# Token lists of a routed expert layer: slots by block and scattered token numbers in place of one-hot matmuls

## The chip, the cores and the metric

One core of a Trainium2 chip runs the whole kernel in one launch. The metric is the device time in microseconds, from the first to the last instruction of the program; lower is better. All times below are of this one core.

## What is computed

The input is x of shape (4, 256, 64, 64), float32. Three modulated deformable 3x3 convolutions (256 to 256 channels, each with a plain 3x3 convolution in front of it that gives two offsets and a mask for each of nine taps) run one after another with a relu, on a copy of x that is normalised over channels; their result is added to x. Then every pixel is a token of 256 values, and a mixture of eight experts is added to it:

```
for wo, bo, w, b in params:                      # three layers
    x = relu(deform_layer(x, wo, bo, w, b))
...
logits = xf @ gate_w + gate_b                    # xf: 16384 tokens, normalised
probs = softmax(logits)
top2_vals, top2_idx = top_k(probs, 2)
...
h = gelu(xf @ w1 + bb1);  y = h @ w2 + bb2       # each expert, hidden size 512
out = out + we[:, None] * y                      # we: the gate of a token, 0 outside its top 2
```

The reference runs each expert on all tokens; the kernel runs an expert only on the tokens that chose it.

## The kernel before, in words

**Blocks and taps.** A block is 512 pixels (eight image rows) of one image and one convolution layer: 3 layers, 4 images and 8 blocks of each make 96 blocks. The list of stages in `run` fixes their order: all of (layer 0, image 0), one block of (0, 1), all of (1, 0), one block of (0, 1), all of (2, 0), then the rest of (0, 1), and so on; a block is named (layer, image, block) here. `main_block` does a block in nine taps. In a tap `samples` issues four gathers from GpSimd (L524; each brings the four corner pixels, 4 KB, for 128 positions), VectorE blends them in two steps (L530, L535), ScalarE scales the result (L538), TensorE transposes it two pairs of samples later (`turn`, L553), ScalarE copies it (L556), and TensorE multiplies it with the tap's weights (`share`, L570). After nine taps ScalarE applies the relu (L601). Nine buffers hold gathered pixels.

**What is woven in.** Everything else is cut into steps, written as generators, and laid between the taps. `step` runs after each tap and advances two lists: `plans_side` holds the offset convolutions (`off_block`, L378 to L448), `side` holds the storing of pixel tables, the preparation of images 2 and 3 (`pre_block`, five steps: load, transpose at L463 and statistics, normalise at L81 and store, transpose back at L483) and the tokens of finished blocks (`tokens`, seven steps). The steps of a list are spread over what is left of the block: with n steps left and r taps left, ceil(n / r) are taken. A step marked `after(self.last)` stands behind the newest L535 on its engine, `after(self.gathered)` behind the newest gather on GpSimd's queue, `after(self.turned)` behind the newest transpose on TensorE.

**The expert layer** is cut into five groups: images 0, 1 and 2 whole (32 sets of 128 tokens each), image 3 in two halves. A group passes through three lanes, `routes`, `tiles` and `sums`, each of which holds pieces with a price in taps; `pump` gives every lane one tap of credit after each tap, and a lane pops a piece when it has its price.
- `routes`: when the last block of a group has given its gates, `route` (L714 on) counts the tokens of each expert with two matmuls over all sets, gives each expert whole tiles of 256 tokens and at most one of 128, and each token a slot in the sorted order (`slots`). Then `invert` turns slots into the list of tokens, one set a piece: VectorE makes two one-hot matrices for each of the two choices (L836, L838), and TensorE multiplies them into one PSUM accumulator (`inv`, L842), which is copied to `tok` at L847. Pieces: 0 taps for `route`, 3 for the first set, 0.5 for each of the other sets (31, or 15 in a half), 3 for `begin`.
- `tiles`: for each tile of the list GpSimd fetches the expert's weights if they changed (L861) and the tokens' rows by one indirect gather for 128 tokens (L874); TensorE transposes them and does the two matmuls with a gelu between (L904, L918, L928, L936); VectorE adds the bias (L955), and the result goes to DRAM. A tile of 256 tokens costs 5.0, 6.0, 2.0, 1.5 or 0.0 taps by group (`pace`), one of 128 half of that.
- `sums`: for each set, GpSimd gathers both results of its tokens (L981), VectorE adds them with their gates (L996), TensorE transposes (L1014), and the output is stored.

After the last block, `settle` and `drain` pop what is left without regard to taps: `settle` one step of each list and one piece of tiles in turn, `drain` three pieces of tiles for one tap of credit of the routes and two of the sums.

Of the kernel before, what the change touches and what calls it, by code (L numbers as in the profile page):

```python
# [8 lines left out]
F32 = mybir.dt.float32  # L9
I32 = mybir.dt.int32  # L10
# [31 lines left out]
NW = 3  # L42
LEAST = 2.0**-30
# [14 lines left out]
def normalise(nc, pool, src, dst, eps, nm):  # L58
# [16 lines left out]
    for _ in range(3):  # L75
        nc.vector.tensor_tensor(sq, rs, rs, ALU.mult)
        nc.vector.scalar_tensor_tensor(sq, sq, -0.5, ve, ALU.mult, ALU.mult)
        nc.vector.scalar_tensor_tensor(rs, sq, 1.5, rs, ALU.add, ALU.mult)
    yield rs
    for t in range(T):  # L80
        nc.vector.tensor_scalar(  # L81
            dst[:, t, :], src[:, t, :], mv[:, t, 0:1], rs[:, t : t + 1], ALU.subtract, ALU.mult
        )


class Group:


    def __init__(self, b, n0, n1):
# [8 lines left out]
        self.zt, self.acc, self.gy, self.sums, self.py = {}, [], [], [], None  # L98
        self.order = [self.starts[s % NW] + s // NW for s in range(self.NF)]
# [26 lines left out]
class Weave:  # L126
# [3 lines left out]
    def __init__(self, ctx, tc, ins, out):  # L130
# [29 lines left out]
        self.side, self.plans_side = [], []  # L160
# [58 lines left out]
    def ffn_constants(self):  # L219
# [9 lines left out]
        for g in self.groups:  # L229
            g.zd = self.dram.tile([g.M * P, C], F32, name=f"z_{g.nm}", tag=f"z_{g.nm}")  # L230
        self.ys = [
# [28 lines left out]
        self.fresh = {}  # L260
        for M in {g.M for g in self.groups}:
            fresh = cst.tile([P, E, M], F32, name=f"fresh_{M}")
            nc.vector.memset(fresh, 1.0)
            nc.vector.memset(fresh[:, :, 0:1], 0.0)
            self.fresh[M] = fresh
# [10 lines left out]
        self.token = {}  # L276
        for M in {g.M for g in self.groups}:
            assert M * P // 2 <= 2048
            token = cst.tile([P, M], F32, name=f"token_{M}")
            nc.vector.tensor_scalar(  # L280
                token, self.row_f[:, :M], float(P), self.part, ALU.mult, ALU.add
            )
            nc.vector.tensor_scalar(token, token, float(M * P // 2), None, ALU.subtract)
            self.token[M] = token


# [163 lines left out]
    def pre_block(self, b, n, wins, spare, spill=0):  # L450
# [19 lines left out]
        rest = normalise(nc, self.small, h, h, EPS_C, nm)  # L470
# [140 lines left out]
    def tokens(self, b, n, r):  # L611
# [4 lines left out]
        if n == grp.n0:  # L616
            grp.cw = self.rt2.tile([P, 2, grp.M], F32, tag="cw", bufs=3, name=f"cw_{grp.nm}")
            grp.rk = self.rt2.tile([P, E, grp.M], F32, tag="rk", name=f"rk_{grp.nm}")
        xc = self.big.tile([P, CC, BLK], F32, tag="a", name=f"xr_{nm}")
# [32 lines left out]
        rest = normalise(nc, self.small, tok, z, EPS_T, nm)  # L652
# [54 lines left out]
        for i in range(2):  # L707
            w = small("lg", (P, TPB, E))
            nc.vector.scalar_tensor_tensor(w, rk, float(i), pr, ALU.is_equal, ALU.mult)
            nc.vector.tensor_reduce(grp.cw[:, i, m0 : m0 + TPB], w, AX.X, ALU.add)  # L710
        if n == grp.n1 - 1:
            self.enqueue(grp)

    def route(self, grp):  # L714
# [6 lines left out]
        def small(tag, shape, dt=F32):  # L721
            return self.rt.tile(list(shape), dt, tag=tag, name=f"{tag}_{grp.nm}")

        both = small("r0", (P, E, M))
        nc.vector.tensor_scalar(both, grp.rk, 1.0, None, ALU.is_le)
        rp = self.ps.tile([P, 2, E, M], F32, tag="tp", name=f"rp_{grp.nm}")
        nc.tensor.matmul(rp[:, 0], lhsT=self.upper, rhs=both, start=True, stop=True)
        nc.tensor.matmul(rp[:, 1], lhsT=self.ones, rhs=both, start=True, stop=True)
        tot = small("r1", (P, E, M))
        nc.vector.tensor_copy(tot, rp[:, 1])  # L730
        slot = small("r2", (P, E, M))
        nc.vector.tensor_tensor_scan(
            slot.rearrange("p e m -> p (e m)"),
            self.fresh[M].rearrange("p e m -> p (e m)"),
            tot.rearrange("p e m -> p (e m)"),
            0.0, ALU.mult, ALU.add,
        )

        ni = small("ni", (P, E), I32)
        nc.vector.tensor_scalar(ni, slot[:, :, M - 1], float(P - 1), None, ALU.add)  # L740
# [8 lines left out]
        for v in range(2):  # L749
# [11 lines left out]
        cut = small("cut", (P, E))  # L761
        nc.vector.tensor_scalar(cut, nt[:, 0], float(FT), None, ALU.mult)
        nc.vector.tensor_tensor(off[:, 1], off[:, 1], cut, ALU.subtract)
        nc.vector.tensor_tensor(off[:, 1], off[:, 1], off[:, 0], ALU.subtract)
        nc.vector.tensor_scalar(end[:, 0], end[:, 0], float(FU), None, ALU.mult)
        nc.vector.tensor_scalar(end[:, 1], end[:, 1], base, None, ALU.add)
        nc.vector.tensor_tensor(slot, slot, tot, ALU.subtract)
        nc.vector.tensor_tensor(slot, slot, rp[:, 0], ALU.add)
        every = [P, E, M]
        over = small("r1", (P, E, M))  # L770
        nc.vector.tensor_tensor(over, slot, cut.unsqueeze(2).to_broadcast(every), ALU.is_ge)
        nc.vector.tensor_tensor(
            over, over, off[:, 1].unsqueeze(2).to_broadcast(every), ALU.mult
# [3 lines left out]
            slot, slot, off[:, 0].unsqueeze(2).to_broadcast(every), ALU.add  # L777
# [9 lines left out]

# [6 lines left out]
        part = small("exv", (P, NF))  # L794
        for v in range(2):
            past = small("r1", (P, NF, E))
            nc.vector.tensor_tensor(
                past,
                first.unsqueeze(2).to_broadcast([P, NF, E]),
                end[:, v].unsqueeze(1).to_broadcast([P, NF, E]),  # L800
                ALU.is_ge,
            )
            nc.vector.tensor_reduce(part if v else ex, past, AX.X, ALU.add)
        nc.vector.scalar_tensor_tensor(ex, ex, float(E), ex, ALU.is_lt, ALU.mult)
        nc.vector.tensor_tensor(ex, ex, part, ALU.add)
# [9 lines left out]
        nc.vector.tensor_copy(grp.wrow, rows)  # L815


        grp.digits = []
        for v, (op, k) in enumerate(((ALU.bitwise_and, P - 1), (ALU.logical_shift_right, 7))):
            di = small("di", (P, 2, M), I32)  # L820
            nc.vector.tensor_scalar(di, grp.slots, k, None, op)
            df = small(f"df{v}", (P, 2, M))
            nc.vector.tensor_copy(df, di)
            grp.digits.append(df)
        grp.inv = self.ps1.tile([P, grp.NU], F32, tag="py", name=f"inv_{grp.nm}")

    def invert(self, grp, m):


        nc = self.nc  # L830
        lo, hi = grp.digits
        n = grp.NU
        for i in range(2):
            nm = f"{grp.nm}_{m}_{i}"
            at = self.ffn.tile([P, P], F16, tag="at", name=f"at_{nm}")
            nc.vector.tensor_scalar(at, self.row_f, lo[:, i, m : m + 1], None, ALU.is_equal)  # L836
            num = self.ffn.tile([P, n], F16, tag="num", name=f"num_{nm}")
            nc.vector.tensor_scalar(  # L838
                num, self.row_f[:, :n], hi[:, i, m : m + 1], self.token[grp.M][:, m : m + 1],
                ALU.is_equal, ALU.mult,  # L840
            )
            nc.tensor.matmul(  # L842
                grp.inv, lhsT=at, rhs=num,
                start=(m == 0 and i == 0), stop=(m == grp.M - 1 and i == 1),
            )
        if m == grp.M - 1:
            nc.vector.tensor_scalar(  # L847
                grp.tok, grp.inv, float(grp.M * P // 2), None, ALU.add
            )
# [176 lines left out]
    def enqueue(self, grp):  # L1026

        put = self.routes.put
        put(0, lambda: self.route(grp))
        for m in range(grp.M):  # L1030
# [181 lines left out]
```

## Time and profile before

| | us |
|---|---|
| median of 3 runs (lowest, highest) | 6431.33 (6419.34, 6440.2) |
| the profiled execution: its own time | 6426.59 |
| the profiled execution: span of its instructions | 6424.5 |

| engine | busy us (share of the span) |
|---|---|
| PE, matmuls | 5903.1 (92%) |
| DVE (VectorE) | 4954.5 (77%) |
| POOL (GpSimd) | 4396.0 (68%) |
| PEld, weight loads | 3413.5 (53%) |
| ACT (ScalarE) | 3298.7 (51%) |

2247.56 MB pass through the DMA engines, at a mean of 350 GB/s. A busy share is a mean over the span. The profile also gives the busy time of every engine, the TensorE clock that was granted, the DMA engines' busy share and their rate for any stretch of the span, and blocks can be told apart in it by the times of L601, the last instruction of each.

### The profile page before, as it was taken

How to read it: one execution, taken by the hardware profiler on the slowest of the kernel's cores; microseconds unless marked ns; L12 is line 12 of the kernel's file. 1: busy time of each engine (PE TensorE's matmuls, PEld its weight loads, DVE VectorE, ACT ScalarE, POOL GpSimd, SP SyncE). 2: the span in 40 equal slices, each digit the busy share in tenths (PEclk: the TensorE clock that was granted, in tenths of full speed). 3: DMA queues.
4: the chain of work that ended last, by engine and by line, in shares of the span. 5: the costliest groups of instructions: out<-in, count | busy, mean ns of one | idle time of the engine just before them, and what ended most of it. 6: DMA issues, size and time to landing. Idle time of an engine off the chain costs nothing.

```text
span 6424.5 us, 88218 instructions
## 1 busy us (share of the span) xinstructions
PE 5903.1 (92%) x26358; PEld 3413.5 (53%) x26358; DVE 4954.5 (77%) x11575; ACT 3298.7 (51%) x7154; POOL 4396.0 (68%) x4215
## 2 busy tenths in 40 slices
PE   7999999889899999999889999999987999987987
PEld 3444444444455555665445555555643566644675
DVE  7988888888977768888877877778988764678621
ACT  3555555555555555555455555555654544454422
POOL 4666776666777767667777776767777764667644
PEclk8999999899999999999999999999999999999998
DMA  8999999999899999999899999999999996899854
GB/s 286 388 370 378 408 404 401 377 361 365 325 393 372 366 340 399 391 355 364 315 356 366 393 380 352 385 368 380 387 369 345 346 338 235 322 335 341 314 179 145
DMA packets 799851, 2247.56 MB, mean 350 GB/s; under 512 B 102184, under 2 KB 300456, under 8 KB 790544
## 3 DMA queue, kind: packets, MB, share of 16 engines
q0 software_dynamic: 550240, 1971.12, 81.2%
q1 hardware_dynamic: 249136, 270.82, 12.3%
q8 instruction: 212, 3.47, 0.2%
q14 instruction: 263, 2.15, 0.1%
HBM read 2166.72 MB, written 191.81 MB: 367 GB/s over the span
## 4 chain that ended last, share of the span: by engine, by line
PE 67%; DVE 11%; DMA 10%; issue 5%; ACT 4%; POOL 2%; SPq 0%; DVEq 0%; ACTq 0%; POOLq 0%
PE acc L570 33%; PE tp L553 9%; DMA g<-tab,idx 8%; PE ph L918 7%; PE py L936 7%; PE po L378 6%; DVE g L530 4%; DVE s L535 3%; ACT s L538 2%; PE pm L392 1%; POOL g L524 1%; PE lp_tok L642 1%; ACT win L601 1%; PE ftp L904 1%; PE tpv L338 1%
## 5 line engine op out<-in xcount | busy, mean ns | idle before, releaser
L524 POOL DMA_INDIRECT g<-tab,idx x3456 | 3625.0, 1049 | 1553.5 <-issue 595.8
L570 PE MATMUL acc<-sT,wk 128*128 128x512 f32 x6912 | 3319.7, 602 | 3.7 <-ACT r L601 1.9
L530 DVE SCALAR_TENSOR_TENSOR g<-g,cf 128x512 f32<-128x512 f32 x3456 | 2561.0, 744 | 348.6 <-DMA g<-tab,idx 341.1
L535 DVE SCALAR_TENSOR_TENSOR s<-g,cf 128x256 f32<-128x256 f32 x3456 | 1656.9, 482 | 480.5 <-PE tp L553 181.0
L538 ACT ACTIVATE s<-s,cf 128x256 f32<-128x256 f32 x3456 | 1664.0, 509 | 642.2 <-DVE s L535 593.8
L570 PEld LDWEIGHTS acc<-sT,wk 128*128 128x128 f32 x6912 | 1195.8, 194 | 818.0 <-issue 801.3
L556 ACT COPY sT<-tp 128x512 f32<-128x512 f32 x1728 | 1011.3, 586 | 1180.0 <-PE tp L553 1167.1
L553 PEld LDWEIGHTS tp<-ident,s 128*128 128x128 f32 x6912 | 867.8, 143 | 1220.0 <-ACT s L538 684.8
L553 PE MATMUL tp<-ident,s 128*128 128x128 f32 x6912 | 1225.1, 282 | 273.0 <-ACT s L538 269.6
L918 PE MATMUL ph<-fzT,w 128*128 128x256 f32 (+1 forms) x2688 | 590.2, 356 | 13.4 <-ACT fzT L908 10.6
L936 PE MATMUL py<-w,hT 128*128 128x256 f32 x2328 | 583.5, 387 | 16.4 <-ACT hT L928 10.4
L918 PEld LDWEIGHTS ph<-fzT,w 128*128 128x128 f32 x2688 | 450.2, 192 | 126.7 <-ACT hT L928 33.5
L928 ACT ACTIVATE hT<-ph,w 128x256 f32<-128x256 f32 (+1 forms) x672 | 266.2, 442 | 467.1 <-PE ph L918 306.2
L936 PEld LDWEIGHTS py<-w,hT 128*128 128x128 f32 x2328 | 425.4, 192 | 136.4 <-issue 47.3
L874 POOL DMA_INDIRECT zt<-z,tok x291 | 292.7, 1006 | 132.4 <-issue 59.2
L981 POOL DMA_INDIRECT gy<-ys,slots x256 | 276.6, 1081 | 105.5 <-issue 65.9
L955 DVE TENSOR_TENSOR y<-py,w 128x512 f32<-128x512 f32 (+1 forms) x168 | 103.3, 615 | 305.2 <-PE py L936 296.7
L861 POOL DMA_INDIRECT w<-in_W,wrow x168 | 177.8, 1059 | 216.9 <-ACT hT L928 45.9
L378 PE MATMUL po<-win,wo 128*32 128x504 f32 (+2 forms) x2560 | 323.8, 551 | 1.5 <-ACT om L387 0.7
L996 DVE SCALAR_TENSOR_TENSOR ta<-gy,cw,ta 128x256 f32<-128x256 f32 x256 | 121.6, 479 | 106.5 <-DMA gy<-ys,slots 87.1
L378 PE MATMUL po<-win_pre,wo 128*32 128x504 f32 (+2 forms) x1280 | 172.0, 572 | 4.0 <-ACT om L387 3.4
L378 PEld LDWEIGHTS po<-win,wo 128*32 128x32 f32 x2560 | 73.1, 109 | 192.0 <-issue 150.1
(171 smaller groups left out, 2836.4 us busy)
## 6 DMA issues: line engine op xcount, KB each, us to landing
tab<-hv SPq DMA_DIRECT2D x512, 128.0 KB
g<-tab,idx POOLq DMA_INDIRECT x3456
tab<-h_pre SPq DMA_DIRECT2D x128, 256.0 KB
ys<-y SPq DMA_DIRECT2D x123, 256.0 KB
wk<-in_conv_w SPq DMA_DIRECT2D x117, 256.0 KB
xc_pre<-in_x SPq DMA_DIRECT2D x32, 512.0 KB
xr_tok<-in_x SPq DMA_DIRECT2D x32, 512.0 KB
t<-t_tok SPq DMA_DIRECT2D x32, 512.0 KB
```

Source lines behind the costliest of these rows:

```text
L378: nc.tensor.matmul(po[g * Q : (g + 1) * Q, :].rearrange("q (r w) -> q r w", w=W)[:, r0:r1, x0:x1], lhsT=self.wo[l][:, 3 * ky + kx, c, :], ...
L524: self.gathered = nc.gpsimd.indirect_dma_start(out=g.rearrange("p x s f -> p (x s f)"), out_offset=None, in_=self.table(*self.stages[i][:2 ...
L530: nc.vector.scalar_tensor_tensor(g[:, :, 0, :], g[:, :, 1, :], cf[:, j, 0:1], g[:, :, 0, :], ALU.mult, ALU.add,)
L535: self.last = nc.vector.scalar_tensor_tensor(s, g[:, 1, 0, :], cf[:, j, 1:2], g[:, 0, 0, :], ALU.mult, ALU.add)
L538: nc.scalar.activation(s, s, AF.Copy, scale=cf[:, j, 2:3])
L553: self.turned = nc.tensor.transpose(tp[:, c, u * P : (u + 1) * P], ss[u][:, c * P : (c + 1) * P], self.ident)
L556: nc.scalar.copy(self.sT[:, :, t0 * P : (t0 + 2) * P], tp)
L570: nc.tensor.matmul(self.acc[:, o, :], lhsT=self.wk[k][:, c, o * P : (o + 1) * P], rhs=sT[:, c, :], start=(k == 0 and c == 0), stop=(k == K ...
L874: self.nc.gpsimd.indirect_dma_start(out=zt, out_offset=None, in_=grp.zd, in_offset=bass.IndirectOffsetOnAxis(ap=grp.tok[:, j : j + 1], axi ...
L918: nc.tensor.matmul(ph[:, h, :n], lhsT=w1[:, o : o + P], rhs=zT[:, c, :n], start=(c == 0), stop=(c == CC - 1),)
L936: nc.tensor.matmul(py[:, u, :], lhsT=hT[h // 2][:, h % 2, u * P : (u + 1) * P], rhs=w2[:, h * C : (h + 1) * C], start=(h == 0), stop=(h == ...
L981: self.nc.gpsimd.indirect_dma_start(out=g, out_offset=None, in_=self.ys[grp.i % 3], in_offset=bass.IndirectOffsetOnAxis(ap=grp.slots[:, i, ...
```

## The change

1. Each expert gets a region of 4096 entries in a table in DRAM (`ids`; two tables in turn). After the gates of a block, a new generator `place` (six steps, in a list of its own, `place_side`) counts that block's tokens per expert with two small matmuls, adds the running count `full`, and writes the numbers of the block's tokens into their experts' regions: eight indirect DMAs of GpSimd, each with 128 destinations of 4 bytes, in two steps of four.
2. `route` works out tiles from `full`, moves slots from the regions to the sorted order, works out which 128 entries of `ids` each unit of the list reads, and reads all of them by one indirect gather; one transpose gives `tok`. It is a generator in six pieces, of 0, 1, 1, 1, 1 and 1 taps; `begin` costs 1 tap. `invert`, its one-hot matrices and its matmuls are gone.
3. The normalising step of `pre_block` runs on ScalarE (a scale and a bias for each position) once the startup is over; in the startup, and for the tokens, it stays on VectorE.
4. `pre_block` steps get a list of their own (`pre_side`), one step a tap. `settle` empties the new lists too.
5. The paces become 6.0, 7.5, 2.4, 1.5 and 0.0 taps.

The diff, cut to its core:

```
-def normalise(nc, pool, src, dst, eps, nm):
+def normalise(nc, pool, src, dst, eps, nm, scalar):
...
+    if scalar:
+        away = pool.tile([P, T], F32, tag="away", name=f"away_{nm}")
+        nc.vector.scalar_tensor_tensor(away, mv[:, :, 0], -1.0, rs, ALU.mult, ALU.mult)
     yield rs
     for t in range(T):
...
+        if scalar:
+            nc.scalar.activation(
+                dst[:, t, :], src[:, t, :], AF.Identity,
+                bias=away[:, t : t + 1], scale=rs[:, t : t + 1],
+            )
...
+        for ids in self.ids:
+            nc.gpsimd.dma_start(ids.rearrange("(p a) b -> p (a b)", p=P), nought)
...
+        self.aside(6, self.place(grp, n), place=True)
+
+    def place(self, grp, n):
...
+        both = small("lg", (P, E, TPB))
+        with self.after(self.last):
+            nc.vector.tensor_scalar(both, rk, 1.0, None, ALU.is_le)
+        yield
+        rp = self.ps.tile([P, 2, E, TPB], F32, tag="tp", name=f"rp_{nm}")
+        with self.after(self.turned):
+            nc.tensor.matmul(rp[:, 0], lhsT=self.upper, rhs=both, start=True, stop=True)
+            nc.tensor.matmul(rp[:, 1], lhsT=self.ones, rhs=both, start=True, stop=True)
+        up = small("rp", (P, 2, E, TPB))
+        nc.scalar.copy(up, rp)
+        yield
+        cs = small("pr", (P, E, TPB))
+        with self.after(self.last):
+            nc.vector.tensor_tensor_scan(
...
+        for t in range(TPB):
+            if t % 2 == 0:
+                yield
+            for i in range(2):
+                with self.after(self.gathered):
+                    ins = nc.gpsimd.indirect_dma_start(
+                        out=ids,
+                        out_offset=bass.IndirectOffsetOnAxis(ap=put[:, i, t : t + 1], axis=0),
+                        in_=self.token[:, m0 + t : m0 + t + 1],
+                        in_offset=None,
+                    ).ins
...
-    def invert(self, grp, m):
...
-            nc.vector.tensor_scalar(at, self.row_f, lo[:, i, m : m + 1], None, ALU.is_equal)
...
-            nc.tensor.matmul(
-                grp.inv, lhsT=at, rhs=num,
...
+        lists = small("r0", (P, P))
+        with self.after(self.gathered):
+            ins = nc.gpsimd.indirect_dma_start(
+                out=lists[: grp.NU],
+                out_offset=None,
+                in_=self.ids[grp.i % 2].rearrange("(n a) b -> n (a b)", a=P),
+                in_offset=bass.IndirectOffsetOnAxis(ap=line[: grp.NU, 0:1], axis=0),
+            ).ins
...
+            nc.tensor.transpose(tp, lists[: grp.NU, :], self.ident[: grp.NU, : grp.NU])
+        with self.after(self.last):
+            nc.vector.tensor_scalar(grp.tok, tp, float(M * P - 1), None, ALU.min)
...
-        put(0, lambda: self.route(grp))
-        for m in range(grp.M):
-            put(0.5 if m else 3, lambda m=m: self.invert(grp, m))
-        put(3, lambda: self.begin(grp))
+        gen = self.route(grp)
+        for taps in range(6):
+            put(min(1, taps), lambda: next(gen, None))
+        put(1, lambda: self.begin(grp))
...
-        for side, taps in ((self.plans_side, K), (self.side, 4 if short else K)):
+        for side, taps in (
+            (self.plans_side, K), (self.side, 4 if short else K), (self.pre_side, K),
+            (self.place_side, K + k),
+        ):
...
-        for i, (g, pace) in enumerate(zip(self.groups, (5.0, 6.0, 2.0, 1.5, 0.0))):
+        for i, (g, pace) in enumerate(zip(self.groups, (6.0, 7.5, 2.4, 1.5, 0.0))):
...
-                        self.aside(5, self.pre_block(1, m, rows.setdefault((-1, 1), {}), True))
+                        gen = self.pre_block(1, m, rows.setdefault((-1, 1), {}), True)
+                        self.aside(5, gen, pre=True)
```

## The prediction

> **What bounds the kernel now.** I read the page first, then the busy time by stage, with block ends taken from L601's times, then the waits and the timeline of the stages that stood out. On the page, PE is busy 92% of the span and the DMA engines close to all of it:
>
> ```profile
> PE   7999999889899999999889999999987999987987
> ...
> DMA  8999999999899999999899999999999996899854
> PE 67%; DVE 11%; DMA 10%; issue 5%; ACT 4%; POOL 2%; SPq 0%; DVEq 0%; ACTq 0%; POOLq 0%
> ```
>
> PE is full in the middle and drops at a few places. The stages, by windows (us, then PE, PEld, DVE, ACT, POOL busy, granted clock, DMA share, GB/s):
>
> ```profile
> 619.00:1018.80 399.80, 370.15 (x1512) 183.60 (x1512) 348.97 (x662) 234.29 (x498) 285.32 (x289) 1.00 1.03 406
> 1186.20:1556.00 369.80, 328.09 (x1396) 182.15 (x1396) 323.52 (x910) 196.61 (x417) 236.25 (x216) 0.91 0.97 363
> 1625.60:1745.00 119.40, 102.84 (x462) 50.06 (x462) 111.29 (x314) 60.37 (x126) 93.50 (x72) 0.97 0.90 326
> 1987.20:2462.10 474.90, 468.81 (x2067) 276.98 (x2066) 354.59 (x671) 256.54 (x578) 339.22 (x330) 1.00 0.97 364
> 3034.90:3250.10 215.20, 174.74 (x766) 88.11 (x766) 185.48 (x543) 97.03 (x203) 164.03 (x134) 0.91 0.89 316
> 3518.30:3977.10 458.80, 451.94 (x1967) 260.55 (x1966) 355.97 (x674) 253.50 (x562) 329.71 (x325) 1.00 0.98 374
> 4450.90:4614.70 163.80, 160.75 (x684) 99.82 (x684) 146.91 (x338) 102.20 (x215) 120.65 (x118) 1.00 1.00 380
> 4725.20:4850.70 125.50, 97.15 (x356) 50.13 (x356) 108.07 (x248) 62.31 (x127) 98.00 (x91) 0.96 0.99 371
> 4725.20:5048.40 323.20, 255.74 (x976) 129.19 (x976) 284.10 (x723) 156.29 (x315) 254.23 (x225) 0.95 0.96 353
> 5774.70:5909.80 135.10, 101.74 (x394) 53.40 (x394) 125.19 (x362) 62.25 (x127) 105.52 (x91) 0.94 0.94 345
> ```
>
> Row 1 is eight blocks of (1,0), convolution alone: 50.0 us a block at a DMA share of 1.03, so DMA-bound, with 46.3 us of PE. Rows 4 and 6 are (1,1) and (1,2), with experts: 59.4 and 57.4 a block, PE at 98.6%, so PE-bound. Row 6 fetches 24 units of 128 tokens, 1.5 tiles a block: a tile of 256 costs (56.5 - 46.3) / 1.5 = 6.8 us of PE. Rows 3, 5, 9 and 10 are stages between experts: lists are made, sums are loaded, and PE stands idle 17, 40, 67 and 33 us at a clock of 0.91 to 0.97. So the expert work is crowded into PE-bound blocks, while other blocks wait for DMA and DVE.
>
> **1. The inverts go.** They are 85.5 + 76.0 us of DVE (L838, L836) and 40.1 of PE (L842), all in these stages. Row 3 is blocks (0,1,3) and (0,1,4): DVE is busy 93%, 41.1 us of it inverts, and they slow the gathers' issue beside them:
>
> ```profile
> 1625.60:1745.00 119.40, 92.09 (x71) 0.97 0.90 326
> 1987.20:2462.10 474.90, 294.44 (x286) 1.00 0.97 364
> ```
>
> That is L524 on POOL: 1.30 us each against 1.03. Without inverts I take such a block at 55 us, near (0,1,1), 55.8. Taking all 41.1 us off would pass the DMA bound of 50. In the new order of the instructions, the first list is read in (0,1,3), and its experts start in (0,1,4), about a block earlier: the way to the experts takes 12 taps (six of `place`, six of the lane) instead of 21.5 (3 + 31 x 0.5 + 3). Row 3: 55 + 55 + two tiles at 2 (below) = 114, **-6**.
>
> **2. Experts are spread.** Counting units of 128 tokens by block in GpSimd's two orders, 25 units (12.5 tiles) move out of PE-bound blocks into (0,1,4), (2,1,7) to (0,2,4) and (2,2,5) to (1,3,1). Between (0,1,5) and (2,1,6) 11 units leave, 5.5 x 6.8 = **-37**; between (1,2,3) and (2,2,5), six units, **-20**. Where they arrive, PE has 5 to 16 us idle a block and pays nothing until that is used (then 6.8 a tile again); DMA pays 256 KB of rows, 256 KB of results and about 0.37 MB of weights (1.18 MB, some 11 changes in 35.5 tiles): 0.9 MB at 400 GB/s, 2.2 us. What the exchange gives can be seen side by side: rows 7 and 8 are blocks of one layer, (2,2,1) to (2,2,3) with 1.67 tiles each, 54.6 us, and (2,2,6), (2,2,7) with sums instead, 62.8.
>
> **3. Sums move.** They follow the tiles, so group 1's leave row 9's blocks for (1,3,3) on, where PE sets the pace (DMA share 0.86 from 5048.4 to 5443.4). Row 9 becomes 54.6 x 2 for (2,2,6) and (2,2,7), about 60 for (1,3,0), 56 for (1,3,1), 53 for (1,3,2), with its inverts gone too: 278, **-45**. At (2,1,7) to (0,2,4), 60.0 and row 5's 215.2: experts now go on there (65, as (2,1,2)), and sums and inverts go: 65 + 72 + 57 + 62 = 256, **-19**. From (0,2,5) to (1,2,2), 433 us, all seven blocks get sums: four at 65, three at 60.5, 441, **+8**. (1,3,3) to (2,3,3) keeps its 71 units; it gains 18 sets of sums, 18 x 0.375 us of L1014 = 7 us of PE, and loses the idle time of its last two blocks: 0. Row 10: no inverts, **-11**; the tail starts some four units ahead: **-5**.
>
> **4. Preparation.** Row 2 is six blocks of (2,0), 61.6 us each, and each has one gap:
>
> ```profile
> 1314.19 1.88 PE L570 MATMUL acc<-sT,wk 128*128 128x512 f32 x4
> 1322.04 1.94 PE L483 MATMUL tp_pre<-ident,h_pre 128*128 128x128 f32 x8 [5.96 <-DVE h_pre L81]
> ```
>
> In the old order, L81 and L483 fall in one tap, because tokens and preparation share a list of 12 steps. The new order has 24 transposes L553 between the forward and the backward transpose, not 16: half a tap, 3.3 us, more room. Moving L81 itself saves 4 x 0.41 us of DVE and adds four ACT instructions of about 0.6 (L538's 0.51 plus 0.1 for a bias operand, L387's 687 ns against L556's 586); ACT stands at 51%, L483 and the stores on SP's queue wait for ACT then, up to 1 us longer. By the row, 5.96 shrinks by 3.3. The Trainium skill, TensorE: Matmul & The Clock Gate (Part 1), says that an idle window of about 3.4 us halves the clock. The trace agrees (0.51 at 1321.4:1324.8, 0.50 at 1335.1:1341.9), so a gap below it would also spare half of 10.2 us: by the rule 8.4 us a block. But 22 MB a block keep DMA at 0.97, so the block can't fall below about 58 (61.6 x 0.97 / 1.03). From 61.6 I take 58.4, for (2,0,1) to (2,0,7): **-22**.
>
> **5. What is added.** For each of 32 blocks: 13 small DVE operations (L709 201 ns, L710 179, L677 191), 2.4 us, against 1.5 saved by step 4; two small matmuls, about 0.5 us as L642's 272 ns; one ACT copy, 0.19; eight scatters. `route` keeps some 50 small operations, in pieces a tap apart. A scatter takes GpSimd about 1.0 us, whatever the rows' size (L874 1006 ns with 1 KB rows, L861 1059 with 9 KB): 8 us a block on POOL, which has about 20 us free a block in row 2. Four stand together ahead of the next gather, and each waits for the DMA eight places before it: four gathers, 4 x 1.25 us, are still in the rings, as long as the four issues take, so DMA need not run dry. DVE's scan waits for ACT's copy of PE's counts; samples queue behind it. It stands one tap later, and L535 waits for PE today for 1.1 us (181.0 in 159 waits).
>
> What 128 writes of 4 bytes to DRAM cost the rings, no row shows: the smallest DRAM writes here are 1 KB. Below: their bytes, nothing (128 x 4 against a gather's 512 KB). Above: the Trainium skill, DMA: Bandwidth & Descriptors (Latency and other measured facts), gives tiny transfers a round trip of at least some 0.8 us to HBM, and its Specifications make writes under 512 B read-modify-writes. If each scatter held the rings so long, 256 x 0.8 = 205 us. I take 0.8 us for a block in all, near the lower end, since the closest rows (gathers of 1 KB pieces) pass at the rate of the large ones: **+25**. The clearing of `ids` is 256 KB at the start: nothing.
>
> **The sum.** -6 -37 -20 -45 -19 +8 -11 -5 -22 +25 = -132. From the profiled execution, 6426.6 - 132 = 6295; it lies 5 us under the median of the runs, so **6295** stands against either. A check: from 1556 to 5048 PE is idle 213 us; the sum leaves about 110, some 2 us a block, as the PE-bound blocks have now.
>
> **The rivals.** *The spread doesn't pay* (chance 0.19): blocks with sums run at a DMA share of 0.95 to 0.99, so tiles that arrive cost there what they save elsewhere. In favour: (0,2,5) to (0,3,0) have sums and experts, and take 67 us. Then only inverts (-12 for each of three groups, -11 in row 10), step 4 and step 5 count: -47 - 22 + 25 = -44, 6383. Against: rows 7 and 8.
> *Slower: the scatters hold the rings* (0.14). They share the rings with the gathers, whose data the chain waits for. At 0.8 us each they cost 205, not 25: 6475. It decides from (132 + 25) / 256 = 0.61 us a scatter on.
> *It doesn't do what it says* (0.07): DVE's waits in `place` stall the samples and lists come no sooner. At L535's longest wait of 4.9 us in each block, 157 us more, less what overlaps: about 6430, no change.
> The sum itself has 0.60.
>
> **Chances and range.** A measurement can tell about 0.3%, 19 us. Faster by more: the sum, the first rival and a little of the third, 0.81. Within: 0.05. Slower: 0.14. The range reaches down to 6200 (scatters free, -25; the clock's whole gain, -45; two us more in each freed block) and up to 6415, past the first rival; what it leaves out is mostly the scatters' case.
>
> **What would show it.** Right: PE at 97% or more from 1750 to 4900 with no stage under 90%; (2,2,6) and (2,2,7) near 55 us; L483's gap in (2,0) under 3 us at a clock above 0.95; L524 near 1.03 us in (0,1,3). Wrong: DVE waiting longer for gathers just after scatters, block times over 62 us in (2,0), or POOL waits for scatters that hold gathers back. Then the range's upper part, or the second rival, is the case.

## The result and the profile after

| | us |
|---|---|
| before, median of 4 runs | 6429.82 |
| after, median of 4 runs (lowest, highest) | 7331.23 (7323.67, 7332.36) |
| ratio, 95% interval | 1.1406 (1.1392 to 1.1419) |
| the profiled execution after: its time, its span | 7330.78, 7328.6 |

The changed kernel is 901 us slower; the forecast was 135 us faster, and its range ended at 6415. The page after, the busy tenths of TensorE, its clock, the DMA engines and their rate, then the chain that ended last:

```profile
PE   7999996567899997677888999986668999856767
...
PEclk9999998788999998888999999997888999977888
DMA  9999999998999999899899999998898998898975
GB/s 319 388 359 396 409 403 289 217 258 262 334 370 390 367 388 274 218 261 284 291 365 370 388 366 382 373 333 239 230 255 278 335 336 300 242 217 206 265 142 171
...
PE 50%; DMA 25%; DVE 11%; issue 6%; POOL 4%; ACT 4%; DVEq 0%; SPq 0%; POOLq 0%; ACTq 0%
PE acc L583 25%; DMA g<-tab,idx 14%; DMA ids<-token,put 8%; PE tp L566 7%; PE po L391 5%; PE ph L1005 5%; PE py L1023 5%; DVE g L543 4%; DVE s L548 3%; POOL ids L779 2%; POOL g L537 2%; ACT s L551 1%; PE pm L405 1%; DMA zt<-z,tok 1%; ACT win L614 1%
```

DMA went from 10% of the chain to 25%, and the scatters (`ids<-token,put`, where `put` is the tile with a block's destinations) are 8% by themselves. In the slices ahead of the tail where PE falls to 5 or 6, the DMA row still says 8 or 9 while the rate is 206 to 289 GB/s: packets are open and move little. Those slices are the stages that route tokens. By stages (us, then PE, PEld, DVE, ACT, POOL busy, clock, DMA share, GB/s), the rows are (1,0); (2,0,2) to (2,0,7); (0,1,3) and (0,1,4); (1,1); (2,2,1) to (2,2,3); (2,2,6) to (1,3,2):

```profile
612.10:1012.80 400.70, 370.56 (x1512) 183.41 (x1512) 349.16 (x661) 234.39 (x498) 284.88 (x289) 1.00 1.03 407
1183.70:1746.50 562.80, 359.02 (x1416) 188.28 (x1416) 340.77 (x959) 206.18 (x446) 282.06 (x266) 0.80 0.90 239
1829.70:1975.70 146.00, 118.12 (x467) 62.29 (x467) 102.17 (x246) 64.66 (x137) 98.73 (x98) 0.91 0.92 319
2209.30:2660.90 451.60, 447.41 (x1961) 258.44 (x1960) 355.76 (x675) 249.97 (x562) 332.89 (x325) 1.00 1.00 381
...
4862.30:5125.60 263.30, 179.27 (x659) 106.37 (x660) 159.81 (x381) 102.63 (x213) 136.20 (x132) 0.81 0.91 248
...
5303.60:5714.20 410.60, 296.00 (x1105) 168.72 (x1105) 256.07 (x602) 168.06 (x347) 243.97 (x237) 0.85 0.90 268
```

Blocks without scatters do what was forecast: (1,0) is unchanged, and (1,1) takes 451.6 where it took 474.9. Most blocks with eight scatters take 80 to 130 us where they took 53 to 91: six blocks of (2,0) 562.8 for 369.8. VectorE's wait for gathers before (us in total, times, longest), then the waits after, and then what the trace says of the scatter's line:

```profile
DVE g L530 <- DMA g<-tab,idx: 341.1, 406, 10.8
```

```profile
DVE g L543 <- DMA g<-tab,idx: 1383.1, 613, 28.4
...
POOL g L537 <- DMA ids<-token,put: 317.3, 63, 13.4
...
POOL ids L779 <- DVE put L772: 196.8, 30, 11.4
```

```profile
L779 POOL DMA_INDIRECT ids<-token,put x256: 967/992/1482, 1181.8 to 7028.1; - x128
...
  DVE put L772: 196.8, 30
  DMA ids<-token,put: 179.2, 48
```

VectorE waited 341.1 us for gathers before, at most 10.8 at a time; now 1383.1, up to 28.4. The issue of a scatter takes the 1.0 us that was assumed (median 992 ns). Three new waits stand beside it: gathers wait on GpSimd for scatters to land, scatters wait for scatters, and in 30 of the 32 blocks that scatter GpSimd waits for the scatter's indices, 6.6 us on average.

### The profile page after: what moved, and what is told of

It reads as the page before. It is cut to its first block, busy times and chain, and to the rows that moved or that the text cites. A ratio compares the mean times of both kernels' runs of the same rounds, so it can differ in the third digit from the quotient of the medians.

```text
span 7328.6 us, 88233 instructions
## 1 busy us (share of the span) xinstructions
PE 6058.4 (83%) x26215; PEld 3470.0 (47%) x26215; DVE 4931.1 (67%) x11385; ACT 3361.0 (46%) x7294; POOL 4569.5 (62%) x4478
## 4 chain that ended last, share of the span: by engine, by line
PE 50%; DMA 25%; DVE 11%; issue 6%; POOL 4%; ACT 4%; DVEq 0%; SPq 0%; POOLq 0%; ACTq 0%
PE acc L583 25%; DMA g<-tab,idx 14%; DMA ids<-token,put 8%; PE tp L566 7%; PE po L391 5%; PE ph L1005 5%; PE py L1023 5%; DVE g L543 4%; DVE s L548 3%; POOL ids L779 2%; POOL g L537 2%; ACT s L551 1%; PE pm L405 1%; DMA zt<-z,tok 1%; ACT win L614 1%
## 5 line engine op out<-in xcount | busy, mean ns | idle before, releaser
L537 POOL DMA_INDIRECT g<-tab,idx x3456 | 3538.4, 1024 | 1809.4 <-issue 632.2
L543 DVE SCALAR_TENSOR_TENSOR g<-g,cf 128x512 f32<-128x512 f32 x3456 | 2569.6, 744 | 1390.7 <-DMA g<-tab,idx 1383.1
L583 PE MATMUL acc<-sT,wk 128*128 128x512 f32 x6912 | 3397.9, 615 | 8.2 <-ACT r L614 5.8
L566 PE MATMUL tp<-ident,s 128*128 128x128 f32 x6912 | 1263.7, 287 | 798.1 <-ACT s L551 786.9
L566 PEld LDWEIGHTS tp<-ident,s 128*128 128x128 f32 x6912 | 892.9, 147 | 1806.8 <-ACT s L551 1229.9
L583 PEld LDWEIGHTS acc<-sT,wk 128*128 128x128 f32 x6912 | 1231.7, 199 | 894.5 <-issue 872.2
L1005 PE MATMUL ph<-fzT,w 128*128 128x256 f32 (+1 forms) x2688 | 617.3, 366 | 32.9 <-ACT fzT L995 18.6
L1023 PE MATMUL py<-w,hT 128*128 128x256 f32 x2328 | 600.3, 391 | 37.0 <-ACT hT L1015 20.3
L779 POOL DMA_INDIRECT ids<-token,put x256 | 267.4, 1045 | 437.7 <-DVE put L772 196.8
L1068 POOL DMA_INDIRECT gy<-ys,slots x256 | 257.4, 1005 | 144.8 <-issue 68.6
L995 ACT COPY fzT<-ftp 128x512 f32<-128x512 f32 (+1 forms) x168 | 89.0, 530 | 207.7 <-PE ftp L991 204.4
```

Of the source, the lines that this page charges most:

```text
L537: self.gathered = nc.gpsimd.indirect_dma_start(out=g.rearrange("p x s f -> p (x s f)"), out_offset=None, in_=self.table(*self.stages[i][:2 ...
L543: nc.vector.scalar_tensor_tensor(g[:, :, 0, :], g[:, :, 1, :], cf[:, j, 0:1], g[:, :, 0, :], ALU.mult, ALU.add,)
L566: self.turned = nc.tensor.transpose(tp[:, c, u * P : (u + 1) * P], ss[u][:, c * P : (c + 1) * P], self.ident)
L583: nc.tensor.matmul(self.acc[:, o, :], lhsT=self.wk[k][:, c, o * P : (o + 1) * P], rhs=sT[:, c, :], start=(k == 0 and c == 0), stop=(k == K ...
L779: ins = nc.gpsimd.indirect_dma_start(out=ids, out_offset=bass.IndirectOffsetOnAxis(ap=put[:, i, t : t + 1], axis=0), in_=self.token[:, m0 ...
L1005: nc.tensor.matmul(ph[:, h, :n], lhsT=w1[:, o : o + P], rhs=zT[:, c, :n], start=(c == 0), stop=(c == CC - 1),)
```

## The experiments

Three theories were set against each other first: (1) writes of neighbouring 4-byte words hold up the memory; (2) any write of a few bytes does; (3) scatters clog GpSimd's queue. The rival to all three: the new order of the work is bad in itself. The runs were made on five chips: c and d below on chips that take about 6430 us for the kernel before, as in the result; x, a and b on chips that take 7465 to 7557. So ratios are to the kernel before on the same chip.

**No scatters** (x1, a2, c2). The table is filled once; the lists' real content is left out.

```
-        nc.vector.memset(nought, 0.0)
+        nc.vector.tensor_scalar(nought, count, 4.0, None, ALU.mult)   # count: slot mod 1024
...
-                    ins = nc.gpsimd.indirect_dma_start(out=ids, ...)
+                pass
```

> The changed kernel without its 256 scatters; the table of lists is filled once at the start with token numbers spread evenly (4 x (slot mod 1024)), so the lists' real content is left out and the outputs are not the reference's, while rows, experts and sums move as many bytes. Everything else of the change stays: slots by block, lists read by one gather, lists during the next routing. If the scatters alone cost the time (theory 1, 2 or 3), it takes about 6270 us: my sum without its +25. If the new order of the work is itself bad (the rival that the spread doesn't pay, or worse), it stays well above 6383, up to 7331.

> The kernel without scatters and with lists filled once at the start (the lists' real content is left out), again, beside the changed kernel on one chip. It was at 0.984 of the kernel before. On a chip where the kernel before takes about 6430 us my sum without its +25 gives 6270, ratio 0.975; the rival that the spread doesn't pay gives 0.989.

> The kernel without scatters (lists filled once, real content left out) beside the kernel before on one chip. 0.985 as in the first two runs on a slow chip; on a chip that takes 6430 us for the kernel before, my sum without its +25 gives 0.9756, the rival that the spread doesn't pay 0.989. By stages, against the kernel before on the same chip: (2,2,6) to (1,3,2) about 45 us less, (1,1) and (2,1) to (2,1,6) 37 us less, (2,1,7) to (0,2,4) 19 us less, (2,0,1) to (2,0,7) 22 us less.

0.9844 (0.9814 to 0.9873), 0.986 (0.981 to 0.9909) and, on a chip like the first, 6302.97 us, 0.9799 (0.9785 to 0.9812). The kernel before was profiled beside that last run:

> The kernel before, unaltered, for its profile on the chip of the runs beside it: the chips of the last three calls took 7465 to 7557 us for it, 16 to 18% more than 6430. If TensorE's signals come late there as in the other kernels on those chips (a fifth of them by 1.5 us and more), this explains its extra 1040 us, and the blocks of this profile can be set beside those of the kernel without scatters, step by step.

That took 6418.76 us (one run). TensorE's signals are on time there (the last section tells of the other chips). So the rival falls: without scatters the new order gains. The scatters cost 7331 - 6303 = 1028 us, 4.0 us each, and the rest of the change is a gain of 129 us by the medians (6431.87 - 6302.97). The same stages without scatters, (2,0,2) to (2,0,7); (1,1); (2,2,6) to (1,3,2):

```profile
1188.90:1556.70 367.80, 326.20 (x1416) 175.42 (x1416) 328.67 (x956) 204.54 (x446) 239.73 (x217) 0.95 0.97 367
...
1976.00:2427.60 451.60, 447.42 (x1961) 258.50 (x1960) 357.39 (x678) 249.76 (x562) 332.02 (x327) 1.00 1.00 382
...
4665.90:4969.70 303.80, 271.09 (x1105) 160.17 (x1105) 254.80 (x603) 165.02 (x346) 206.06 (x201) 0.96 0.94 355
```

**Words far apart, and reads instead of writes** (x2, x3). x2 writes the same numbers 512 bytes apart into a table that nobody reads; x3 reads 128 words in place of each scatter. Both keep the filled lists of x1.

```
x2: +        nc.vector.tensor_scalar(put, sf, 128.0, None, ALU.mult)
x2: +                        out=self.wide, out_offset=...(ap=put[:, i, t : t + 1], axis=0),
x3: +                        out=back[:, i, t : t + 1], in_=ids, in_offset=...(ap=put[...], axis=0),
```

> The kernel of x1 with its 256 scatters again, the same numbers written, but into a table of its own with 512 bytes between slots, so no two words share a line of memory; nothing reads them (content of the lists as in x1). Theory 1 (writes to neighbouring words of one line are serialised): close to x1, at most 6270 + 256 x 0.2 = 6320 us. Theory 2 (any write of a few bytes costs this, wherever it goes): about 7330. Theory 3 (scatters clog GpSimd's queue): about 7330 too, x3 tells it from theory 2.

> The kernel of x1 with each scatter turned into a gather of 128 words of 4 bytes at the same indices, from the table into SBUF, issued at the same places on GpSimd's queue; the data are not used (content of the lists as in x1). Issue time, number of descriptors and places in the queue are those of the scatters, and only the direction is turned. Theory 3 (queue, issue, descriptors): about 7330 us. Theories 1 and 2 (writes to memory): 6270 to 6330.

1.0593 (1.0559 to 1.0627) and 1.0616 (1.0583 to 1.0649), against 0.9844 beside them. Both lie between the outcomes that were set out (about 0.98 and 1.14), so no theory holds alone. Some 560 to 590 us on that chip don't depend on the direction: theory 2 falls as far as it blamed writes, and this part fits theory 3. The reads of x3 go to the places that the changed kernel writes, 4 bytes apart, and cost no more than far writes. So the further price that neighbouring words have below belongs to writing them.

**Words 32 bytes apart** (x4, a3, c4), the complete kernel, beside the changed kernel itself (a1).

```
-        nc.vector.tensor_copy(put, sf)
+        nc.vector.tensor_scalar(put, sf, 8.0, None, ALU.mult)
-                in_=self.ids[grp.i % 2].rearrange("(n a) b -> n (a b)", a=P),
+                in_=self.ids[grp.i % 2].rearrange("(n a) b -> n (a b)", a=8 * P),
```

> The changed kernel, complete, with slots 32 bytes apart in the table instead of 4: the scatter's indices are multiplied by 8, and the gather of the lists reads 4 KB per unit (71 x 4 KB for a large group) of which every eighth word is used. Theory 1 with a line of 32 bytes: about 6300 us, faster than both kernels. Theory 1 with lines of 64 bytes or more: between, as fewer words share a line, some 6400 to 6900. Theories 2 and 3: about 7330.

> The changed kernel, unaltered, as the anchor for the runs beside it: the chip that ran the four kernels before this one took 7471 us for the kernel before (6430 elsewhere), so all figures here are ratios to the kernel before on the same chip. 1.14 if what the change costs is the same on every chip. If neighbouring words cost something of their own (theory 1 beside the queue's cost, which the far words and the tiny reads showed at 1.06), it lies above 1.065 on any chip; if theory 1 has no part, at 1.06 where the far words are at 1.06.

> The complete changed kernel with slots 32 bytes apart, again, beside the changed kernel on one chip. The distance to the changed kernel is what neighbouring words cost, the distance to the kernel without scatters what the rest of a scatter costs (its wait for its indices on GpSimd, its issue, its descriptors). Theory 1 alone would put it at 0.98; after the first runs I expect both parts, some 1.06, with the changed kernel at 1.10 to 1.14.

> The complete changed kernel with slots 32 bytes apart. On a slow chip 1.0635 as before. On a chip that takes 6430 us for the kernel before, where the changed kernel took 1.1406: if the split is the same there, neighbouring words cost about 430 us and this takes 6900, ratio 1.073; if neighbouring words cost all of it there, about 6300, ratio 0.98.

On the chip of x2 and x3 this is at 1.0639 (1.0604 to 1.0675). On another the changed kernel is at 1.1224 (1.1176 to 1.1272) and this at 1.0635 (1.0588 to 1.0681); on a chip like the first it is at 1.0436 (1.042 to 1.0452), 6710.64 us, against 1.1406. The one change is the spacing (and 4 KB read in place of 512 bytes for each unit of a list), and it takes off 433 us on the one and 621 us on the other: theory 1 has its part, and a larger one on the faster chip than I had expected. Going on from 32 bytes to the 512 of x2 changes little (1.0639 and 1.0593), though x2's lists are filled and x4's real: so the filled lists of the runs without real content don't decide either. VectorE's wait for gathers follows the same order: 341 us before, 361 without scatters (c2), 770 with words 32 bytes apart (c4), 1383 in the changed kernel. The trace shows how. Five-microsecond windows of the changed kernel around the eight scatters of one block, issued from 1283.6 to 1306.9 (columns as above):

```profile
1288.00:1293.00 5.00, 4.49 (x15) 2.00 (x13) 1.97 (x9) 1.11 (x3) 3.85 (x4) 1.00 0.62 43
1293.00:1298.00 5.00, 0.00 (x0) 0.00 (x0) 0.00 (x0) 0.00 (x0) 2.01 (x2) 0.88 2.23 52
1298.00:1303.00 5.00, 0.00 (x0) 0.00 (x0) 0.00 (x0) 0.00 (x0) 0.97 (x1) 0.50 0.91 10
1303.00:1308.00 5.00, 0.00 (x0) 0.00 (x0) 0.00 (x0) 0.00 (x0) 0.97 (x1) 0.50 0.00 0
...
1318.00:1323.00 5.00, 4.96 (x34) 3.71 (x32) 0.00 (x0) 1.31 (x3) 0.00 (x0) 1.00 1.32 51
1323.00:1328.00 5.00, 0.00 (x0) 0.00 (x0) 0.00 (x0) 0.00 (x0) 0.69 (x1) 0.61 0.98 31
1328.00:1333.00 5.00, 0.00 (x0) 0.00 (x0) 0.00 (x0) 0.00 (x0) 1.19 (x2) 0.50 0.62 85
```

With words 32 bytes apart (c4), the eight of the next block in the order are issued from 1337.4 to 1351.9:

```profile
1342.00:1347.00 5.00, 3.66 (x14) 1.66 (x12) 1.78 (x9) 0.73 (x2) 3.81 (x4) 1.00 0.39 119
1347.00:1352.00 5.00, 2.54 (x5) 1.34 (x6) 3.46 (x12) 1.50 (x3) 3.95 (x4) 0.77 0.60 196
1352.00:1357.00 5.00, 4.50 (x20) 2.34 (x18) 2.24 (x4) 3.39 (x8) 3.89 (x4) 0.89 0.45 151
1357.00:1362.00 5.00, 3.12 (x27) 2.64 (x25) 1.28 (x3) 1.81 (x5) 3.78 (x5) 1.00 0.95 305
1362.00:1367.00 5.00, 3.18 (x6) 1.64 (x7) 3.35 (x6) 2.27 (x5) 4.09 (x4) 0.66 1.04 413
```

In the first the rate stays at 0 to 107 GB/s for 45 us, but for one window between, and TensorE, VectorE and ScalarE stand still through three windows in a row. The DMA share is 2.23 in one window and 0 two windows later, since a packet's time and bytes both count where it starts. Laid out over their own time, 16 packets are open without a break from 1293 to 1308, as many as there are DMA engines: the 76 packets that start from 1293 to 1303, all of 4 KB, take up to 14.3 us, and none starts from 1303 to 1308. In the second the share falls with the rate (the rings, from which the DMA engines take their packets, are short of work at 119 to 196 GB/s), and 413 GB/s are back 10 us after the last scatter. By the packets of all blocks, a 4 KB packet that starts within 30 us after a scatter takes a mean of 453 ns in the changed kernel and 179 ns with words 32 bytes apart. The median is 159 in both: the mean comes from one packet in ten that takes over 1 us (up to 16.7), where with words apart it is one in 280 (up to 2.1). The scatter's own packets take a mean of 14 ns in both.

**Scatters later** (a4, b4, d2). Two empty steps between `put` and the scatters, two scatters a tap over four taps: with words 32 bytes apart (a4, d2) and 4 (b4).

```
+        yield
+        yield
         for t in range(TPB):
-            if t % 2 == 0:
-                yield
+            yield
```

> The complete changed kernel with slots 32 bytes apart and its scatters two taps after the indices are made (two empty steps ahead of them), two at a time in four taps instead of four at a time in two. If the queue's part is GpSimd waiting for the indices (the tiny reads wait 7.7 us for them in each block, while gathers stand behind them), it falls by about 32 x 8 = 250 us against the kernel with slots 32 bytes apart, ratio about 1.02; if it is the scatters' issue and descriptors, it stays within 0.01 of that kernel.

> The complete changed kernel, slots 4 bytes apart as it has them, with the scatters two taps later and two at a time in four taps. Where slots were 32 bytes apart this took 129 us off (1.0635 to 1.046). If the price of neighbouring words is a fixed one per word, the same comes off here: 1.122 - 0.017 = 1.105. If it is a jam that builds up when four scatters of one block meet in the memory, spacing them in time takes more off: 1.07 to 1.09.

> The complete changed kernel with slots 32 bytes apart and its scatters two taps later, two at a time. On a slow chip it was at 1.046 against 1.0635 without the delay. On a chip that takes 6430 us, where slots 32 bytes apart gave 1.0436, I expect the same 0.017 off: 1.027. If what stays is the rings' share of a scatter, it can't fall below the 0.98 of the kernel without scatters plus 256 x 1 us: 1.02.

1.0462 (1.0408 to 1.0515), 1.0871 (1.0829 to 1.0914) and, on a chip like the first, 6502.63 us, 1.0102 (1.0086 to 1.0118): 208 us less there, more than I expected, and below the 1.02 that I had called a floor. With neighbouring words the delay takes off more, 0.035 (1.1224 to 1.0871, two chips) where it took 0.017 with words apart (1.0635 to 1.0462). This fits a jam that builds up when scatters meet, forecast at 1.07 to 1.09, and not a fixed price for each word, forecast at 1.105. The delay and the spreading over four taps were not tried one without the other. GpSimd's wait for the indices is gone (idle before the scatters, 32 bytes apart, at once and later):

```profile
L781 POOL DMA_INDIRECT ids<-token,put x256 | 270.9, 1058 | 270.9 <-DVE put L774 192.7 <-issue 66.5 <-DVE s L550 9.3
```

```profile
L782 POOL DMA_INDIRECT ids<-token,put x256 | 272.9, 1066 | 81.1 <-issue 66.9 <-DMA g<-tab,idx 5.2 <-DMA ids<-token,put 4.0
```

**What else a scatter costs** (b1, b2, b3, all with filled lists). b1 issues only the first scatter of each pair; b2 puts a copy on GpSimd that reads the same indices in place of each scatter, with no transfer; b3 writes 16 words in place of 128.

```
b1:  for i in range(1):
b2:  nc.gpsimd.tensor_copy(self.idle, put[:, i, t : t + 1].to_broadcast([P, 384]))
b3:  ap=put[:16, i, t : t + 1]    in_=self.token[:16, m0 + t : m0 + t + 1]
```

> The kernel with far words (512 bytes apart, lists filled once so that their real content is left out), with only the first of the two scatters of each tile of tokens: 128 scatters instead of 256, at the same places. Of the 560 us that the 256 cost there (ratio 1.059 against 0.985 without), half go if each scatter has its own price (issue, descriptors, its place in the queue): ratio 1.022. If the price is mostly the wait for the indices ahead of the first scatter of a block, it stays above 1.04.

> The kernel without scatters (lists filled once, real content left out), with each scatter's place on GpSimd taken by a copy of 384 words that reads the scatter's indices: the same wait for the indices and some 0.5 to 1 us of GpSimd, but no transfer. If the far words' price is GpSimd's time and its wait, the ratio is 1.04 to 1.06; if it is the transfers (descriptors in the rings, one of the places among outstanding transfers), only the wait stays, some 130 us as the later scatters showed: 1.00 to 1.005.

> The kernel with far words (lists filled once, real content left out), each scatter writing 16 words instead of 128: same number of scatters, same waits, an eighth of the descriptors. If descriptors set the price, 560 / 8 = 70 us stay with the wait's 130: ratio about 1.01. If issue and wait set it, as the far words: 1.05 to 1.06.

1.0313 (1.0284 to 1.0341), 1.0114 (1.0079 to 1.0148) and 1.0659 (1.0632 to 1.0687). They are set against x1 and x2, which ran on another chip (0.9844 and 1.0593), so differences under some 0.01 say nothing. An eighth of the words costs no less than all of them, so far words are priced by the transfer and not by the word. The traces, counted against x1, fit: each scatter leaves 32 packets either way, 16 of 32 bytes (eight words) and 16 of 4 bytes in x2, 32 of 4 bytes in b3. Half the transfers keep 0.047 of 0.075: more than half, so it seems that a part comes once in a block. The copy fell between its two forecasts. It keeps the wait (248.8 us for `put`, 256.5 in x2) and stays 0.027 above no scatters; the other 0.05 need a transfer.

```profile
L785 POOL CAST idle<-put 128x384 f32<-128x384 int32 x256 | 162.0, 633 | 249.9 <-DVE put L778 248.8
```

The copy is shorter than a scatter's issue (633 ns against 1066 in x2), so 0.4 us of GpSimd in each is part of those 0.05; the runs don't part it from the rings.

**Parts of the change alone** (c3, d1): preparation in its own list and on ScalarE, in the kernel before; then also the new paces, lists still by one-hot products.

```
c3: +        rest = normalise(nc, self.small, h, h, EPS_C, nm, not self.starting)
c3: +            ... (self.pre_side, K),
d1: +        zip(self.groups, (6.0, 7.5, 2.4, 1.5, 0.0))
```

> The kernel before with one part of the change alone: preparation in a list of its own and normalised on ScalarE (step 4 of the sum); lists are made by the old one-hot products, nothing is scattered. My step 4 says 22 us less, ratio 0.9966; if preparation brings nothing, 1.000; if it brings all that the kernel without scatters gains on a slow chip, 0.985.

> The kernel before with preparation in a list of its own and the change's wider spacing of expert tiles (6.0, 7.5 and 2.4 taps instead of 5.0, 6.0 and 2.0), lists still by one-hot products, no scatters. If the gain of the kernel without scatters (0.980) comes from the spacing of the experts, most of it is here without any scatter: some 60 us less than before, ratio 0.990. If it comes from lists that are ready a block earlier, the experts only end later here: 0.998 to 1.005.

0.9982 (0.9975 to 0.9988) and 6362.21 us, 0.9889 (0.9876 to 0.9903). The second beats both kernels: 74 us less than before with nothing scattered, 12 by the preparation (c3) and the other 62 by the paces. In (2,0) the transpose back, L483 of the kernel before, now waits 1.17 us in place of 5.96 (c3):

```profile
1324.18 1.67 PE L493 MATMUL tp_pre<-ident,h_pre 128*128 128x128 f32 x6 [1.17 <-ACT h_pre L85]
1326.28 0.64 PE L493 MATMUL tp_pre<-ident,h_pre 128*128 128x128 f32 x2
```

## Why the prediction was wrong, by its steps

**The step that failed is 5**, the price of the scatters: "I take 0.8 us for a block in all, near the lower end ... **+25**". In its place stand 1028 us for the scatters alone. On chips that take 6430, the parts taken off one after the other:

| part of the scatters' price | from | us | each |
|---|---|---|---|
| neighbouring words (4 bytes against 32) | 7331 - 6711 | 620 | 2.4 |
| wait for the indices, and four in a bunch | 6711 - 6503 | 208 | 0.8 |
| what a scatter apart and later still costs | 6503 - 6303 | 200 | 0.78 |

The sizes depend on the order: with neighbouring words the delay takes off twice as much, as b4 showed.

The last row has the size that I had as the upper bound: 256 x 0.8 = 205, from the Trainium skill's round trip to HBM (DMA: Bandwidth & Descriptors, Latency and other measured facts). That is luck. The page gives the round trip as a floor for tiny transfers, and I used it as a ceiling; no run here has a scatter's round trip.

Three errors led past the bound.
- I chose the low end because gathers with 1 KB pieces pass at the rate of large ones. But the profile before has no packet of 1 KB in GpSimd's queue: it has 461200 of 4096 bytes, and rows of 1 KB go four to a packet. So no row was near 4 bytes, and a far row is no reason to leave the only bound.
- The upper bound priced a scatter by its own time in the rings, and its packets are indeed short (14 ns). What it does to the packets behind it (453 ns for 179) was in neither end, so the interval did not hold the cost.
- "four gathers, 4 x 1.25 us, are still in the rings, as long as the four issues take, so DMA need not run dry" left out GpSimd's wait for `put`, 6.6 us ahead of the scatters, with the next gathers behind them on the same queue. I had named VectorE's wait for ScalarE in `place`, not this one.

The second rival named the place and the signs (VectorE waiting longer for gathers just after scatters, over 62 us in (2,0), GpSimd's waits for scatters) and the resource that is shared. It lacked both larger parts, the neighbouring words and the wait for the indices; its size was a fifth of the real one, so the range missed as well.

**The other steps**, with the scatters gone: blocks of c2 against c1, one chip, block ends by the last instruction of each block. These are single executions, and c1's lies 13 us under the median of the kernel before, c3's 15 us above its own: a row can be off by several us.

| step (us, sums of blocks in the profiled executions) | predicted | measured |
|---|---|---|
| 1: (0,1,3), (0,1,4), inverts | -6 | +4 |
| 2: (0,1,5) to (2,1,6), experts leave | -37 | -42 |
| 2: (1,2,3) to (2,2,5) | -20 | -15 |
| 3: (2,2,6) to (1,3,2), sums move | -45 | -18 |
| 3: (2,1,7) to (0,2,4) | -19 | -18 |
| 3: (0,2,5) to (1,2,2) | +8 | +21 |
| 3: (2,3,4), (2,3,5); tail | -11; -5 | +3; -52 |
| 4: (2,0,1) to (2,0,7), alone (c3) | -22 | -17 |
| 4 with `place` beside it (c2) | | +3 |
| (0,1,2), first stages, (1,3,3) on | 0 | -0.4 |
| all, without the scatters | -157 | -114 |

Step 2 was right to 6 us a row, so the first rival (the spread doesn't pay) falls. d1 shows that it is the paces, and not the earlier lists: with the preparation they bring -37 and -20 in these two rows. Step 3 was right in sign except at the end, where the experts reached (2,3,5), and the gain came in the tail; at (2,2,6) to (1,3,2) it was less than half of the forecast.

Step 1 missed. The inverts slowed the gathers' issue as I had read: 79.68 us for 80 gathers in (0,1,3) and (0,1,4) after, 1.00 us each for 1.30. But the two blocks got no shorter without scatters, 124.6 us at a DMA share of 0.96; what holds them was not looked into.

```profile
1829.70:1975.70 146.00, 79.68 (x80) 0.91 0.92 319
```

Step 4's gap shrank as the row said (5.96 to 1.17, blocks of (2,0) near 58), and the clock rose from 0.90 (c1) to 0.98 (c3) in (2,0,2) to (2,0,7). The trace bears out only one of the two halved stretches that step 4 shows: ahead of the second, from 1335.1, TensorE's longest pause since the gap is 0.82 us, so no gap explains it. In c2 the gain is gone: -17 against +3 in seven blocks, 2.8 us a block. The transpose back waits 1.17 us there too, but TensorE has a new wait, for VectorE's compare in `place` (L746) ahead of its count (L750). From 1300 to 1556, five blocks of (2,0), it is (us in total, times, longest)

```profile
PE rp L750 <- DVE lg L746: 14.4, 5, 3.4
```

That is 2.9 us a block, where step 5 had 0.5 us for both small matmuls and no wait; c3 has no such row. So TensorE's wait for VectorE went from one matmul to another. That this wait is the whole of the loss is read from the two sizes; `place` without it was not tried.

What is not settled: why neighbouring words jam the memory. That they share a line or a row there, and are written by different DMA engines, was only argued; a list written by one engine was not tried. Words 32 bytes apart also lie in a table eight times as large, and the runs don't part the one from the other. The last 200 us are not parted either, into GpSimd's issue and what the packets do.

## What to carry to other kernels

Before a per-element scatter to DRAM goes into a kernel that lives on gathers, measure it beside the gathers: its own packets and its issue tell nothing of what it does to the packets behind it. If it must be, keep the words 32 bytes or more apart (nothing between 4 and 32 was tried), issue it after its indices are surely there, and count some 0.8 us for each, as here. And take a change apart before building it: the tiles' spacing, one line, and the preparation had 74 of the 129 us that all but the scatters brought.

## What the runs showed that I had not expected

- Neighbouring 4-byte writes by indirect DMA stop other traffic: packets that start in 5 us carry 10 GB/s and none start in the next 5, where some 400 GB/s are usual.
- A scatter of 16 far words costs as much as one of 128 (1.0659 and 1.0593), and 128 reads of neighbouring words as much as 128 writes of far ones (1.0616).
- On the chips that take 7465 us and more for the kernel before, ScalarE waits for TensorE's signals with no instruction that ends near them (the kernel without scatters there, waits of ScalarE); the profile of the kernel before on a chip that takes 6430 has no such row. By the semaphores' times, for about a fifth of TensorE's signals there the next update on record comes over 1.5 us after the modelled end, up to 37 us; on the other chips for at most seven in 5025. But the record there also holds fewer updates than signals (4045 for 5035 without scatters; 5037 for 5035 on the other kind of chip), so late ones and unrecorded ones are not told apart. The cause is open.

```profile
ACT sT L574 <- PE tp L571: 1197.5, 957, 7.2
ACT sT L574 <- remote: 522.5, 139, 14.4
```
